# A deformable convolution by shifted products: edge tiles without unasked columns, and a reordered first image

## The chip, the cores and the metric

The kernel runs on one core of one Trainium2 chip, in one launch. The metric is device time in microseconds (us). A profile of one execution stands beside the run times; its engines are PE (TensorE, matmuls; PEld is its weight load), DVE (VectorE), ACT (ScalarE), POOL (GpSimd) and SP (SyncE, which here only issues DMAs). An engine name with a q, as in SPq, is the engine's queue that issues a DMA.

## The reference

The input x has 8 images of 128 channels and 64 x 64 pixels, all float32. Two layers follow each other.

```python
# layer 0
xn   = group_norm(x)                                  # 32 groups
om   = conv3x3(xn, off_w) + off_b                     # 27 maps: 9 taps x (dy, dx), 9 masks
mask = sigmoid(om[:, 18:])
val  = bilinear sample of xn at (row + ky - 1 + dy, col + kx - 1 + dx), per tap, times mask
y    = einsum('bckhw,ock->bohw', val, w) + b
x    = x + relu(batch_norm(y) * gamma + beta)
# layer 1
xn   = group_norm(x)
out  = sum over the two best of four experts (gated per image) of conv3x3(xn, expert) + shared conv3x3(xn)
x    = x + out
```

The change lies in layer 0 alone.

## The kernel before

**Sampling by matmul.** Offsets are assumed to be under 2 pixels (`REACH = 2`; a general path, guarded by a count at the end, is not taken with these inputs). The bilinear weight of a neighbour at distance d is then max(0, 1 - |dy - d|) times the same in x, a "tent", with 5 tents (`NR`) in each direction. The padded image of 66 x 66 sample positions is cut into 11 bands of 6 rows (`NT1`, `T`), and a band into 11 tiles of 6 columns. For one tile, the 10 x 10 source pixels that can matter (`QQ = 100`) stand on the partitions, and the 9 taps x 6 rows x 6 columns = 324 sample positions on the free axis.

- `pick` (L508, L516, ACT) copies the 10 x 10 patches of a band; `pixels` (L529, L536) transposes them on PE into `xt`, pixels by channels.
- `weights` (L546, DVE) multiplies `x_wts` and `y_wts`, the tents of the 100 pixels, into `s` (100 x 324).
- `sample` (L557, PE) multiplies `xt` by `s` into `pq` (128 channels x 324), and ACT (L563) copies it into `samples`, of shape (tap, 8 rows, 66 columns). Two rows are carried to the next band by L665.
- `conv` (L572, PE) adds up 9 products of 6 x 64 columns in `py`, one for each tap, with the tap's 128 x 128 weights. The first band of an image has 4 rows, so 256 columns.
- `finish` (L583, L586) adds the bias, takes statistics and stores the rows.

A float32 matmul is recorded as two instructions; "a pair" below is one such matmul.

**Tables.** `tables(b)` makes the tents of one image: it loads x (L245), normalises it (L257 to L286), computes the offset convolution (L312 to L373) with 32-column products, stores the 27 maps to DRAM by rows (`rowwise`, L378) and, for the x offsets, by columns (`colwise`, after the copy `omc` of L375, stored by L382), loads them shifted by tap into `off_y`, `mask` (L397) and `off_x` (L405), takes the Sigmoid (L413), computes five tents for y (L458 to L463, DVE) and x (L453, L460, ACT), and stores them into `y_table` (L433) and `x_table` (L441). `load_y` (L476) and `load_x` (L492) load a band's tents, 6 and 10 DMAs, into one of two y and three x buffers.

**Order.** The order on every engine is written out by hand. `tables` is a generator; image 0's tables run alone at the start, and those of later images are interleaved, a step or two for each tile, with the band loop. In the loop, at each tile: `weights` three tiles ahead, `sample`, a load for the band after next (from POOL's queue), one tap of `conv` of the band before, and a piece of `pixels` of the next band. At the start the queues are: SP loads x, the offset weights (L596), their bias (L598, four copies) and other constants; POOL clears buffers and combines the offset weights (L612 to L616), then computes the power for `scale` (L279); DVE clears buffers (L391) after the offsets are out. After the tables of image 0, `load_y(0)`, `load_x(0)` (spread over SP, ACT and POOL), `load_y(1)` and `load_x(1)` are issued, then `pick` and `pixels`, and the band loop begins.

Layer 1 (L1159 is its matmul) follows the band loop of all images; its lines do not change.

Of the kernel before, what the change touches and what calls it, by code (L numbers as in the profile page):

```python
# [57 lines left out]
def deform_moe_conv(  # L58
# [110 lines left out]
    def dense():  # L169

        with ExitStack() as st:
# [34 lines left out]

            combos = [a1.tile([P, H // 2, W], F32, name=f"combo{i}") for i in range(2)]
# [6 lines left out]
            )  # L214
            off_x = flat[0:WB, 2 * YSTEP : 2 * YSTEP + TAPS * (WP6 - 1) + ROWPAD]


            x_wts = [a1.tile([P, NT1, T, TAPS, T], F32, name=f"xwts{i}") for i in range(3)]
            y_wts = [a1.tile([P, T, TAPS, WB], F32, name=f"ywts{i}") for i in range(2)]
# [3 lines left out]
            samples = [a1.tile([P, TAPS, T + 2, WB], F32, name=f"samples{i}") for i in range(2)]  # L223
            dw_sb = a1.tile([P, TAPS, P], F32, name="dw_sb")
            ystats = a1.tile([P, B, NT1, 6], F32, name="ystats")
            ymvs = a1.tile([P, B, 2], F32, name="ymvs")
            xts, ss = {}, {}
            bands = [(b, j) for b in range(B) for j in range(NT1)]

            def tables(b):  # L230
# [11 lines left out]
                others = (nc.sync, nc.sync) if b else (nc.scalar, nc.gpsimd)  # L242
# [132 lines left out]
                nc.scalar.copy(omc, omr.rearrange("p (h w) -> p w h", w=W))  # L375
                yield from pause(4)
                for j in range(4):
                    nc.sync.dma_start(  # L378
                        out=rowwise[b][:, j * HW // 4 : (j + 1) * HW // 4],
                        in_=omr[32 * j : 32 * j + 27],  # L380
                    )
                    others[j % 2].dma_start(  # L382
                        out=colwise[b][:, :, H // 4 * j : H // 4 * (j + 1)],
                        in_=omc[32 * j + 9 : 32 * j + 18],
                    )
# [3 lines left out]
                if b == 0:  # L389
                    for t in (y_wts[1], x_wts[1], x_wts[2]):  # L390
                        nc.vector.memset(t, 0.0)  # L391
                yield from pause(9)
                for k in range(3):
                    rows = slice(k, k + H)
                    for t, c in ((off_y, 3 * k), (mask, 2 * TAPS + 3 * k)):
                        one = t[rows, 0, k, 0:1]
                        nc.sync.dma_start(  # L397
                            out=bass.AP(
                                tensor=one.tensor, offset=one.offset,
                                ap=[list(one.ap[0]), [3 * WB + 1, 3], [1, W]],  # L400
                            ),
                            in_=rowwise[b][c : c + 3].rearrange("s (h w) -> h s w", w=W),
                        )
                    one = off_x[rows, k * 3 * (WP6 - 1) + ROWPAD :]
                    others[k % 2].dma_start(  # L405
                        out=bass.AP(
                            tensor=one.tensor, offset=one.offset,
                            ap=[list(one.ap[0]), [WP6, 3], [1, H]],
                        ),
                        in_=colwise[b][k::3].rearrange("s w h -> w s h"),  # L410
                    )
# [3 lines left out]
                if b:  # L415
                    work = a1.tile([WB, 2, 2, YSTEP], F32, name="work", tag="om")
                    tents = [[work[:, a, i % 2] for i in range(NR)] for a in range(2)]
                else:
                    tents = []
                    for t in samples:  # L420
                        flat = t.rearrange("p k r w -> p (k r w)")
                        tents.append(
                            [flat[0:WB, i * YSTEP : (i + 1) * YSTEP] for i in range(NR)]
                        )
# [3 lines left out]
                    ap=[list(one.ap[0]), [T, NT1], [WP6 - 1, TAPS], [1, T]],  # L428
                )

                def store(i):
# [8 lines left out]
                    )  # L440
                    nc.sync.dma_start(  # L441
# [8 lines left out]
                for i in range(NR):  # L450
                    ty, tx = tents[0][i], tents[1][i]
                    step = steps[0:WB, i : i + 1]
                    nc.scalar.activation(  # L453
                        tx.rearrange("p (n k j) -> p n k j", n=NT1, j=T), by_bands, AF.Abs, bias=step
                    )

                    dy, at = off_y.rearrange("p u v j -> p (u v j)"), REACH - i
                    nc.vector.tensor_scalar(ty, dy, -1.0, float(1 - at), ALU.mult, ALU.add)  # L458
                    yield
                    nc.scalar.activation(tx, tx, AF.Relu, bias=1.0, scale=-1.0)  # L460
                    nc.vector.scalar_tensor_tensor(ty, dy, float(1 + at), ty, ALU.add, ALU.min)
                    yield
                    nc.vector.scalar_tensor_tensor(  # L463
                        ty, ty, 0.0, mask.rearrange("p u v j -> p (u v j)"), ALU.max, ALU.mult
                    )
                    if i:
                        store(i - 1)
                    yield from pause(2)
                store(NR - 1)

            def load_y(g, r, engine):

                if g >= len(bands):
# [3 lines left out]
                    out=y_wts[g % 2][r * Q : (r + NR) * Q, r].rearrange("p b c -> p (b c)"),  # L477
# [62 lines left out]
            def weights(n):  # L540

                if n >= len(bands) * NT1:
                    return
                g, c = divmod(n, NT1)
                s = a6.tile([P, TAPS, T, T], F32, name="s")
                nc.vector.tensor_tensor(  # L546
                    s[0:QQ],
                    x_wts[g % 3][0:QQ, c].rearrange("p a k r -> p k r a"),
                    y_wts[g % 2][0:QQ, :, :, T * c : T * c + T].rearrange("p r k a -> p k r a"),
# [4 lines left out]
            def sample(n):  # L554
                g, c = divmod(n, NT1)
                pq = ps_q.tile([P, TAPS, T, T], F32, name="pq")
                nc.tensor.matmul(  # L557
                    pq.rearrange("p k r a -> p (k r a)"),
                    lhsT=xts[g][0:QQ, c],
                    rhs=ss.pop(n)[0:QQ].rearrange("p k r a -> p (k r a)"),  # L560
                    start=True, stop=True,
                )
                nc.scalar.copy(samples[g % 2][:, :, 2 : T + 2, T * c : T * c + T], pq)  # L563

            def conv(g, i, py):
# [4 lines left out]
                n = 3 * kx + ky  # L570
# [4 lines left out]
                    rhs=samples[g % 2][:, n, first + ky : T + ky, kx : kx + W],  # L575
# [20 lines left out]
            nc.sync.dma_start(out=offw_sb[:, :, 0:27], in_=off_w)  # L596
            for j in range(4):
                nc.sync.dma_start(  # L598
                    out=offb_sb[32 * j : 32 * j + 27], in_=off_b.rearrange("a s -> s a")
                )  # L600
            def reach():
# [5 lines left out]
                count = a1.tile([1, 1], F32, name="count")  # L607
                nc.vector.tensor_reduce(count, pn[0:1], AX.X, ALU.add)
                nc.vector.tensor_copy(count_i, count)
# [12 lines left out]
            for _ in made:  # L622
                pass
            for r in range(T):
                load_y(0, r, nc.gpsimd)
            for q in range(Q):
                load_x(0, q, (nc.sync, nc.scalar, nc.gpsimd)[q % 3])
# [4 lines left out]
            for g in range(2):  # L632
                pick(g)
            for _ in pixels(0):
                pass
# [4 lines left out]
            for g in range(len(bands) + 1):  # L640
# [8 lines left out]
                for c in range(NT1):  # L649
# [14 lines left out]
                    if c == 1 and j:  # L664
                        nc.scalar.copy(  # L665
                            samples[g % 2][:, :, 0:2], samples[(g - 1) % 2][:, :, T : T + 2]
# [578 lines left out]
```

## Time and profile before

| what | value |
|---|---|
| median of 3 runs | 1708.23 us (1705.34 to 1708.29) |
| the profiled execution's own time | 1705.5 us |
| its span | 1703.8 us |
| mean granted clock of TensorE | 0.973 |
| first product of `weights` | 75.49 us after the span's start |
| band loop, to the last `conv` | to about 1317 us |

The page's busy shares are over the whole span; its slices are 1/40 of it, 42.6 us each. In a group's line the time after the bar is the busy sum and the mean of one instruction in ns, then the engine's idle time just before these instructions and what ended it. In a timeline the columns are start, duration (both us), engine, line, operation, tiles, and how many were merged.

### The profile page before, as it was taken

What the parts mean: (1) busy time and instruction counts of PE and PEld (TensorE: products, weight loads), DVE (VectorE), ACT (ScalarE), POOL (GpSimd) and SP (SyncE); (2) the same over time, 40 slices, a digit from 0 to 9 for tenths busy, and PEclk for the clock granted to TensorE, in tenths of its full rate; (3) what the DMA queues carried; (4) which work ended last, traced back from release to release, by engine and by line L of the source; (5) the groups of instructions that cost most, each with busy time, mean ns of one, the idle gap of its engine ahead of it and who ended that gap; (6) DMA issues with size and microseconds to landing.
All of it is one profiled execution on the core that took longest, in us unless ns stands there. A gap on an engine that the chain in (4) does not pass through costs nothing. (4 is left out here: it accounts for less than half of the span.)

```text
span 1703.8 us, 20572 instructions
## 1 busy us (share of the span) xinstructions
PE 1591.8 (93%) x6106; PEld 918.3 (54%) x6106; DVE 1280.1 (75%) x1990; ACT 954.9 (56%) x1970; POOL 938.3 (55%) x1518
## 2 busy tenths in 40 slices
PE   3299999999999999999999999999999479999998
PEld 1155565666566556656665665566665234444443
DVE  6586777678687868776786878686664888888882
ACT  1465765776576667657765766676664423333320
POOL 3375576658667757766686676667771412222210
PEclk9599999999999999999999999999999689999999
DMA  4644864685477457647854775675762624444111
GB/s 133 128 119 113 166 169 114 143 183 132 112 159 183 115 120 184 154 114 141 192 125 110 161 183 126 129 162 133 171 149 53 266 87 155 158 153 149 76 63 52
DMA packets 197598, 235.82 MB, mean 138 GB/s; under 512 B 133964, under 2 KB 148048, under 8 KB 197478
## 3 DMA queue, kind: packets, MB, share of 16 engines
q0 software_dynamic: 94976, 124.94, 33.4%
q1 hardware_dynamic: 100556, 109.04, 21.6%
q8 instruction: 54, 0.88, 0.2%
q10 hardware_dynamic: 1946, 0.41, 0.1%
q14 instruction: 66, 0.54, 0.1%
HBM read 183.00 MB, written 50.82 MB: 137 GB/s over the span
## 5 line engine op out<-in xcount | busy, mean ns | idle before, releaser
L546 DVE TENSOR_TENSOR s<-xwts,ywts 100x324 f32<-100x324 f32 x968 | 706.6, 761 | 205.3 <-PE pq L557 172.3
L557 PE MATMUL pq<-s,xt 100*128 100x324 f32 x1936 | 693.5, 440 | 6.0 <-DVE s L546 6.0
L563 ACT COPY samples<-pq 128x324 f32<-128x324 f32 x968 | 425.1, 443 | 410.1 <-PE pq L557 403.5
L572 PE MATMUL py<-samples,dw_sb 128*128 128x384 f32 (+1 forms) x1584 | 624.4, 476 | 0.7 <-ACT y L583 0.7
L492 POOL DMA_DIRECT2D xwts<-tabx x863 | 524.7, 618 | 74.0 <-DMA ywts<-taby 35.9
L476 POOL DMA_DIRECT2D ywts<-taby x528 | 302.9, 588 | 337.2 <-DVE s L546 259.6
L557 PEld LDWEIGHTS pq<-s,xt 100*128 100x128 f32 x1936 | 324.5, 190 | 163.5 <-issue 28.7
L572 PEld LDWEIGHTS py<-samples,dw_sb 128*128 128x128 f32 x1584 | 299.9, 189 | 135.1 <-ACT y L583 2.7
L529 PE MATMUL pt<-ident,picked 128*100 128x128 f32 x968 | 194.6, 276 | 44.2 <-ACT picked L516 34.6
L529 PEld LDWEIGHTS pt<-ident,picked 128*100 128x100 f32 x968 | 121.0, 128 | 186.9 <-issue 44.8
L1159 PE MATMUL pc<-v,u 128*128 128x512 f32 x384 | 172.5, 598 | 9.3 <-DVE u L1108 9.3
L1159 PE MATMUL pc<-v,wmix 128*128 128x512 f32 x384 | 176.0, 604 | 0.0
L536 ACT COPY xt<-pt 100x512 f32<-100x512 f32 (+1 forms) x264 | 147.7, 559 | 2.2 <-PE pt L529 2.2
L1159 PEld LDWEIGHTS pc<-v,u 128*128 128x128 f32 x384 | 72.4, 190 | 98.3 <-issue 85.1
L1137 ACT ACTIVATE t<-pc,bmix 128x512 f32<-128x512 f32 x32 | 22.0, 687 | 182.3 <-PE pc L1159 100.3
L586 DVE BATCH_NORM_STATS2 ystats<-y 128x6 f32<-128x384 f32 (+1 forms) x88 | 48.3, 549 | 100.4 <-ACT y L583 100.4
L1159 PEld LDWEIGHTS pc<-v,wmix 128*128 128x128 f32 x384 | 72.3, 191 | 88.4 <-issue 84.7
L508 ACT COPY picked<-pad 128x900 f32<-128x900 f32 x88 | 91.6, 1041 | 9.6 <-DMA xwts<-tabx 9.6
L665 ACT COPY samples<-samples 128x1188 f32<-128x1188 f32 x80 | 95.9, 1199 | 0.0
L987 POOL TENSOR_TENSOR x<-x,xt 128x512 f32<-128x512 f32 x32 | 47.3, 1514 | 85.0 <-ACT x L985 85.0
L312 DVE TENSOR_TENSOR combo<-pad 128x1024 f32<-128x1024 f32 x64 | 77.4, 1227 | 8.5 <-PE pc L329 8.5
L987 POOL TENSOR_TENSOR pad<-pad,pad 128x512 f32<-128x512 f32 x28 | 39.6, 1445 | 71.7 <-ACT pad L985 71.5
(145 smaller groups left out, 998.3 us busy)
## 6 DMA issues: line engine op xcount, KB each, us to landing
ywts<-taby POOLq DMA_DIRECT2D x528, 116.0 KB, 4.2
pad<-in_x_dram SPq DMA_DIRECT2D x48, 512.0 KB
xwts<-tabx POOLq DMA_DIRECT2D x173, 116.0 KB, 4.1
out_dram<-yo SPq DMA_DIRECT2D x32, 512.0 KB
xwts<-tabx POOLq DMA_DIRECT2D x172, 92.8 KB, 4.0
yd<-y SPq DMA_DIRECT2D x80, 192.0 KB
xwts<-tabx POOLq DMA_DIRECT2D x173, 69.6 KB, 3.7
pad<-yd SPq DMA_DIRECT2D x16, 512.0 KB
```

Source lines behind the costliest of these rows:

```text
L476: engine.dma_start(out=y_wts[g % 2][r * Q : (r + NR) * Q, r].rearrange("p b c -> p (b c)"), in_=bass.AP(tensor=y_table[b].tensor, offset=y ...
L492: engine.dma_start(out=x_wts[g % 3][q:QQ:Q, :, lo:hi].rearrange("p t a b c -> p t (a b c)"), in_=bass.AP(tensor=x_table[b].tensor, offset= ...
L508: nc.scalar.copy(picked[g % 2][:, 1 : NT1 - 1], bass.AP(tensor=one.tensor, offset=one.offset, ap=[list(one.ap[0]), [T, NT1 - 2], [W, Q], [ ...
L529: nc.tensor.transpose(pt[0:QQ, c], picked[g % 2][:, c0 + c].rearrange("p y x -> p (y x)"), ident,)
L536: nc.scalar.copy(xts[g][0:QQ, c0 : c0 + n], pt[0:QQ, 0:n])
L546: nc.vector.tensor_tensor(s[0:QQ], x_wts[g % 3][0:QQ, c].rearrange("p a k r -> p k r a"), y_wts[g % 2][0:QQ, :, :, T * c : T * c + T].rear ...
L557: nc.tensor.matmul(pq.rearrange("p k r a -> p (k r a)"), lhsT=xts[g][0:QQ, c], rhs=ss.pop(n)[0:QQ].rearrange("p k r a -> p (k r a)"), star ...
L563: nc.scalar.copy(samples[g % 2][:, :, 2 : T + 2, T * c : T * c + T], pq)
L572: nc.tensor.matmul(py[:, first:], lhsT=dw_sb[:, 3 * ky + kx], rhs=samples[g % 2][:, n, first + ky : T + ky, kx : kx + W], start=(i == 0), ...
L665: nc.scalar.copy(samples[g % 2][:, :, 0:2], samples[(g - 1) % 2][:, :, T : T + 2])
L987: adder.tensor_tensor(y, y, xt[:, c * CH : (c + 1) * CH], ALU.add)
L1159: nc.tensor.matmul(pc, lhsT=us[j][:, kx], rhs=vs[g][:, rows, kx : kx + W], start=(kx == 0), stop=(kx == 2),)
```

## The change

1. **Edge tiles.** In `samples`, `s` and `pq` the order becomes (row, ky, column, kx), with the taps in reversed order, so that a tile is 18 x 18. `asked` cuts off the two outer rows and columns of this square that no output pixel asks for, in the first and last band and in the first and last tile of a band; the matmul and the copy out take only the rest. `conv` reads its tap from the new layout: the moving operand's column step is 3 elements.
2. The tents and their loads follow the new order (`x_wts` as (column, row, tap), `y_wts` as (row, ky, column, kx)). The y tents are computed in a spare part of `combos[0]`, and the third DVE step writes them in the new order. The offset weights and bias come in reversed tap order: loaded raw into `combos[0]`, reversed by 9 + 9 ACT copies, and the bias sent on by four DMAs.
3. **First image.** The `omc` copy is split between ACT and DVE; the `colwise` stores are all issued by POOL, the `off_x` loads all by ACT; a one-element Sigmoid stands first on ACT; each tent is stored as soon as it is made, x ahead of y; the third x buffer is cleared after the tents; `pick(0)` and `pixels(0)` come ahead of the loads; of `load_x(0)` SP issues six, ACT three, POOL one.

```diff
-            x_wts = [a1.tile([P, NT1, T, TAPS, T], F32, name=f"xwts{i}") for i in range(3)]
-            y_wts = [a1.tile([P, T, TAPS, WB], F32, name=f"ywts{i}") for i in range(2)]
+            x_wts = [a1.tile([P, NT1, T, T, TAPS], F32, name=f"xwts{i}") for i in range(3)]
+            y_wts = [a1.tile([P, T, 3, WB, 3], F32, name=f"ywts{i}") for i in range(2)]
...
-            samples = [a1.tile([P, TAPS, T + 2, WB], F32, name=f"samples{i}") for i in range(2)]
+            samples = [a1.tile([P, T + 2, 3, WB, 3], F32, name=f"samples{i}") for i in range(2)]
+            for t in samples:
+                ends = t.rearrange("p r y w x -> p (r y) (w x)")
+                nc.gpsimd.memset(ends[:, 3 * T :, 0:2], 0.0)
+                nc.gpsimd.memset(ends[:, 3 * T :, 3 * WB - 2 :], 0.0)
...
+            nc.scalar.activation(count_f, nhalf[0:1], AF.Sigmoid)
...
-                nc.scalar.copy(omc, omr.rearrange("p (h w) -> p w h", w=W))
+                turned = omr.rearrange("p (h w) -> p w h", w=W)
+                if b:
+                    nc.scalar.copy(omc, turned)
+                else:
+                    nc.scalar.copy(omc[:, 0 : W // 2], turned[:, 0 : W // 2])
+                    nc.vector.tensor_copy(omc[:, W // 2 :], turned[:, W // 2 :])
...
-                others = (nc.sync, nc.sync) if b else (nc.scalar, nc.gpsimd)
+                beside = nc.sync if b else nc.gpsimd
...
-                    others[j % 2].dma_start(
+                    beside.dma_start(
                         out=colwise[b][:, :, H // 4 * j : H // 4 * (j + 1)],
...
-                    others[k % 2].dma_start(
+                    (nc.sync if b else nc.scalar).dma_start(
...
-                        tx.rearrange("p (n k j) -> p n k j", n=NT1, j=T), by_bands, AF.Abs, bias=step
+                        tx.rearrange("p (n j k) -> p n j k", n=NT1, j=T), by_bands, AF.Abs, bias=step
...
                     nc.vector.scalar_tensor_tensor(
-                        ty, ty, 0.0, mask.rearrange("p u v j -> p (u v j)"), ALU.max, ALU.mult
+                        ty.rearrange("p (v j u) -> p v j u", v=3, u=3),
+                        tent_y.rearrange("p (u v j) -> p v j u", u=3, v=3), 0.0,
+                        mask.rearrange("p u v j -> p v j u"), ALU.max, ALU.mult,
                     )
-                    if i:
-                        store(i - 1)
+                    if b == 0:
+                        store_x(i)
+                        store_y(i)
+                    elif i:
+                        store_y(i - 1)
+                        store_x(i - 1)
...
-                    x_wts[g % 3][0:QQ, c].rearrange("p a k r -> p k r a"),
-                    y_wts[g % 2][0:QQ, :, :, T * c : T * c + T].rearrange("p r k a -> p k r a"),
+                    x_wts[g % 3][0:QQ, c].rearrange("p a r (y x) -> p (r y) a x", x=3),
+                    y_wts[g % 2].rearrange("p r y a x -> p (r y) a x")[
+                        0:QQ, :, T * c : T * c + T
+                    ],
...
+                def asked(t, m0):
+                    m1, k0, k1 = m0 + 3 * T, 0, 3 * T
+                    if j == 0:
+                        m0 += 2
+                    if j == NT1 - 1:
+                        m1 -= 2
+                    if c == 0:
+                        k0 += 2
+                    if c == NT1 - 1:
+                        k1 -= 2
+                    return t[:, m0:m1, k0:k1]
+
+                pq = ps_q.tile([P, 3 * T, 3 * T], F32, name="pq")
                 nc.tensor.matmul(
-                    pq.rearrange("p k r a -> p (k r a)"),
+                    asked(pq, 0),
                     lhsT=xts[g][0:QQ, c],
-                    rhs=ss.pop(n)[0:QQ].rearrange("p k r a -> p (k r a)"),
+                    rhs=asked(ss.pop(n)[0:QQ].rearrange("p m a x -> p m (a x)"), 0),
                     start=True, stop=True,
                 )
-                nc.scalar.copy(samples[g % 2][:, :, 2 : T + 2, T * c : T * c + T], pq)
+                rows = samples[g % 2].rearrange("p r y w x -> p (r y) (w x)")
+                nc.scalar.copy(
+                    asked(rows[:, :, 3 * T * c : 3 * T * (c + 1)], 6), asked(pq, 0)
+                )
...
-                    rhs=samples[g % 2][:, n, first + ky : T + ky, kx : kx + W],
+                    rhs=samples[g % 2][:, first + ky : T + ky, 2 - ky, kx : kx + W, 2 - kx],
...
-            nc.sync.dma_start(out=offw_sb[:, :, 0:27], in_=off_w)
+            nc.sync.dma_start(out=raw_w.rearrange("p k s t -> p k (s t)"), in_=off_w)
+            nc.sync.dma_start(out=raw_b.rearrange("p s t -> p (s t)"), in_=off_b)
...
+            for k in range(TAPS):
+                nc.scalar.copy(reversed_w[:, :, :, k], raw_w[:, :, :, TAPS - 1 - k])
+            for k in range(TAPS):
+                nc.scalar.copy(reversed_b[:, :, k], raw_b[:, :, TAPS - 1 - k])
             for j in range(4):
-                nc.sync.dma_start(
-                    out=offb_sb[32 * j : 32 * j + 27], in_=off_b.rearrange("a s -> s a")
-                )
+                nc.sync.dma_start(out=offb_sb[32 * j : 32 * j + 27], in_=offb_row)
...
+            pick(0)
+            for _ in pixels(0):
+                pass
             for r in range(T):
                 load_y(0, r, nc.gpsimd)
             for q in range(Q):
-                load_x(0, q, (nc.sync, nc.scalar, nc.gpsimd)[q % 3])
+                load_x(0, q, (nc.sync, nc.sync, nc.scalar)[q % 3] if q < 9 else nc.gpsimd)
+            pick(1)
             for r in range(T):
                 load_y(1, r, nc.gpsimd)
             for q in range(Q):
                 load_x(1, q, nc.sync)
-            for g in range(2):
-                pick(g)
-            for _ in pixels(0):
-                pass
```

## The prediction

> **What bounds the kernel now.** I read the page's busy table and slices first, then TensorE's timeline inside one band, then the groups of the deform stage by shape, then the timeline of the first 80 us.
>
> ```profile
> PE 1591.8 (93%) x6106; PEld 918.3 (54%) x6106; DVE 1280.1 (75%) x1990; ACT 954.9 (56%) x1970; POOL 938.3 (55%) x1518
> PE   3299999999999999999999999999999479999998
> PEclk9599999999999999999999999999999689999999
> ```
>
> The digits show two places where PE is not full: the first two slices (the first image's tables, up to about 80 us) and the seam near 1320 us before layer 1. A busy digit 9 doesn't prove a full PE, so I look at the order of its starts:
>
> ```profile
> 627.61 0.71 PE L557 MATMUL pq<-s,xt 100*128 100x324 f32 x2
> 628.16 0.81 PE L572 MATMUL py<-samples,dw_sb 128*128 128x384 f32 x2
> 628.81 0.38 PE L529 MATMUL pt<-ident,picked 128*100 128x128 f32 x2
> 629.02 0.71 PE L557 MATMUL pq<-s,xt 100*128 100x324 f32 x2
> 629.57 0.81 PE L572 MATMUL py<-samples,dw_sb 128*128 128x384 f32 x2
> 630.22 0.71 PE L557 MATMUL pq<-s,xt 100*128 100x324 f32 x2
> 630.77 0.81 PE L572 MATMUL py<-samples,dw_sb 128*128 128x384 f32 x2
> ```
>
> Start to start, a pair of pq (324 columns) takes 0.55 us, a pair of py (384 columns) 0.65 us, one transpose 0.11 us. So 60 columns cost 0.10 us: **1.67 ns a column of a pair**, and nothing is left between them. A band has 11 pq, 9 py and 11 pt: 6.05 + 5.85 + 1.2 = 13.1 us, and the same place in the next band is 13.05 us later. In this stage every column removed from PE is time removed from the run, and every nanosecond added per column is added.
>
> ```profile
> L546 DVE TENSOR_TENSOR s<-xwts,ywts 100x324 f32<-100x324 f32 x943 | 689.0, 762 | 186.3 <-PE pq L557 171.5 <-DMA xwts<-tabx 9.5 <-DMA ywts<-taby 2.2
> L563 ACT COPY samples<-pq 128x324 f32<-128x324 f32 x947 | 416.1, 443 | 396.1 <-PE pq L557 389.6
> L665 ACT COPY samples<-samples 128x1188 f32<-128x1188 f32 x79 | 94.7, 1199 | 0.0
> L312 DVE TENSOR_TENSOR combo<-pad 128x1024 f32<-128x1024 f32 x56 | 68.1, 1227 | 6.5 <-PE pc L329 6.5
> L375 ACT COPY om<-om 128x1024 f32<-128x1024 f32 x7 | 14.1, 2011 | 0.0
> ```
>
> DVE and ACT wait for pq, not the other way round. The group also prices strides. L375 reads with a step of 256 bytes: 2011 ns for 1024 elements, 1.96 ns each; L665 reads rows: 1.01 ns each. L546 reads xwts with a step of 216 bytes: 2.35 ns an element; L312 reads rows: 1.20 ns. One element in each distant place costs about double.
>
> ```profile
> 46.54 1.28 ACT L413 ACT_TABLE_LOAD   x1 [11.79 <-DMA combo<-rowwise]
> 57.35 0.29 SPq L433 DMA_DIRECT2D taby<-samples  x1
> 57.74 0.84 SPq L441 DMA_DIRECT2D tabx<-samples  x1
> 61.73 15.48 SPq L492 DMA_DIRECT2D xwts<-tabx  x13
> 62.56 3.43 POOL L476 DMA_DIRECT2D ywts<-taby  x6 [19.70 <-DMA tabx<-samples]
> 75.49 4.73 DVE L546 TENSOR_TENSOR s<-xwts,ywts 100x324 f32<-100x324 f32 x7 [18.16 <-DMA ywts<-taby]
> ```
>
> Before 75.49 us the run is one serial chain: offsets, mask, tents, stores, loads, first product. Each step shortened there counts in full too.
>
> **What the Trainium skill says.** *SBUF — State Buffer*, Door 1, says that SBUF has 16-byte lines, that an engine needs at least two hits per line for full rate, and sums it up as "how far you can stride for free depends on dtype: 4 fp32". The trace agrees far beyond a line (216 and 256 bytes: double). For a step of 12 bytes the two sentences part: it is under 4 fp32, but gives 4 elements in 3 lines, fewer than two hits. No row of before has such a step. *ScalarE: Activation LUTs*, What ACT_TABLE_LOAD costs, gives about 1283 ns; the trace has 1.28 us.
>
> **The change, part by part.**
>
> *Edge products.* A tile's product has 18 rows by 18 columns; edge tiles lose 2 on each outer side. An image's 11 x 11 tiles go from 121 x 324 = 39,204 columns to (198 - 4) squared = 37,636: 1,568 fewer, 12,544 over 8 images, x 1.67 ns = **-20.9 us**, all on the path. The smallest edge product has 256 columns, and py with 256 columns runs in L572 too, so weight loads (190 ns) stay covered. L563 copies 16 x 16 to 18 x 18 elements, never more than before. Rows of 16 out of 18 in PSUM are not contiguous; L329 already writes rows of 63 out of 64 there. Bound: 0 to -21.
>
> *Taps innermost.* To make that rectangle, samples becomes (row, ky, column, kx), so the convolution's moving operand steps 3 floats, **12 bytes**, instead of 1. It streams 36,864 columns an image (10 bands of 9 x 384, one of 9 x 256), 294,912 in all, 492 us. Bounds: 0 if a step under a line is free; if a line takes two element times, 3 lines per 4 elements is 6 times instead of 4: +246 us; doubled as at 216 bytes: +492. Below nothing is excluded: the rows read now are contiguous. I take 0, because the page's summary puts the limit at 4 fp32 and because the doubling is shown only where each element has its own line.
>
> *L546* now reads runs of 3 and 18 instead of a 216-byte step: between 0.43 (324 x 1.2 ns plus its overhead) and 0.76 us. DVE waits for PE there, so it is worth nothing in the steady stage; its cover is PE.
>
> *Tents.* For every image the third DVE tent step reads both inputs with a large step (0.77 up to 1.4 us by the doubling), ACT's Abs as well (0.80 up to 1.3). For images 1 to 7 that is 7 x 5 x 1.1 us beside a full PE, with DVE idle some 20% of the stage: nothing; were DVE full, 39 us.
>
> *First image, early.* Weights come raw and ACT reverses them: 9 copies, then 9 of the bias, at 0.2 us each (two L516 copies take 0.40). The weights land near 9.5 us (SP's beta load at 9.52 had waited for them), so they are ready near 11.3 instead of POOL's start of L612 at 10.46; the pow of `scale` is queued behind on POOL and slips 0.8 us. Four small memsets on POOL lie inside that. The bias is ready near 13.1; SP issues four more DMAs (2.46 us for such four) and they land near 17, while the first combo, due at 16.2, overwrites the raw buffer: 0.8 more. SP's later loads for image 1 slip about 5 us; image 1 is first needed at 82. Together **+1.6** (0 to +3).
>
> *First image, middle.* The Sigmoid table at the start takes 1.28 off 46.54. The omc copy split over ACT and DVE gives colwise 0.9 us, and four colwise stores on POOL instead of two return it (0.94 each); both lie beside SP's six off_y/mask loads, which end last. ACT issues three off_x loads instead of two, 0.7 us, before the Sigmoid it has to wait for anyway. The memset of x_wts[2] moves behind the tents, where DVE waits for loads. Against it five slower third steps, +3.1, move the last y store from 57.35 to 59.2; but now y goes last and x, whose 726 small rows land slowest (57.74 to 61.7), goes earlier. I take **-0.3** (-3 to +2).
>
> *First image, loads.* Before, POOL issues six y loads, then three of the first band's x loads from 65.95 to 68.6, which need about 7 us to land: 75.5. After, POOL has one of these, SP six ahead of the next band's, ACT three behind pick and pixels. The last is issued near 66: first product near 73, **-2.5** (-5 to +1).
>
> Sum: -20.9 + 1.6 - 0.3 - 2.5 = -22.1. The profiled execution took 1705.5 us (span 1703.8), giving 1683.4; the median shown is 2.7 above it, giving 1686. I say 1685.
>
> **Rivals.**
>
> *The 12-byte step is charged.* L572 alone gets slower: at 1.5 times 1705.5 - 22 + 246 = **1930 us**, at double 2175. It decides from 22/492 = 4.5%: a py pair of 0.68 instead of 0.65 us. For it speaks the two-hits sentence; against it that only steps far above a line are seen to cost. 0.18.
>
> *Another engine sets the edge bands.* A top or bottom band shrinks by 0.5 us to about 12.5, POOL issues 16 loads of 0.6 us in it, 9.7, and waits for DVE in between (L476). If half the gain is lost there: **1695 us**. Against: loads are issued two bands ahead. 0.10.
>
> *The first image gets later instead of earlier,* 5 us, by the small copies and slower tents: **1690 us**; speaks for it that they are serial. 0.12. Eaten up altogether, about 1706: 0.03.
>
> **How the numbers follow.** Forecast 0.57, and the two milder rivals 0.10 and 0.12, are all faster by over 0.2% (3.4 us, about what a measurement of this kernel tells from no change): 0.79. No difference 0.03. Slower 0.18. The range 1674 to 1699 takes in the ends of the first image's terms and the half-lost edge gain; the charged step lies outside it.
>
> **What would show it.** Right: pq pairs of 0.48 us at edges (288 columns) and 0.43 at corners, py pairs still 0.65, no table load before the Sigmoid, first L546 product near 73, layer 1 unchanged. Wrong: py pairs over 0.68 us, or PE waiting for POOL's loads in top and bottom bands, or the first combo later than 17 us.

## The result: 1957 us, the opposite of the forecast, and the profile after

| what | before | after |
|---|---|---|
| median of 4 runs | 1707.89 us (1705.34 to 1708.29) | 1957.37 us (1956.06 to 1958.25) |
| ratio after / before | | 1.1464, interval 1.1444 to 1.1484 |
| span of the profiled execution | 1703.8 us | 1956.2 us |
| mean granted clock of TensorE | 0.973 | 0.976 |
| first product of `weights` | 75.49 us | 76.53 us |
| last `conv` of the band loop done | about 1317 us | about 1571 us |

The change costs 249.5 us. The clock is the same, and of the span's 252 us the band loop has all (its end moves by 254). The page of after, the lines that answer to those shown of before:

```profile
PE 1851.2 (95%) x6106; PEld 934.3 (48%) x6106; DVE 1049.1 (54%) x1991; ACT 977.1 (50%) x1988; POOL 935.4 (48%) x1521
...
PE   3499999999999999999999999999999947999998
...
PEclk8699999999999999999999999999999978999999
```

PE is busy 1851 us instead of 1592, with the same 6106 matmul instructions; DVE and POOL have not become busier, and ACT only by 22 us (977 instead of 955). So the time is inside PE's own instructions. PE's timeline inside one band of after shows which:

```profile
700.82 0.72 PE L606 MATMUL pq<-s,xt 100*128 100x324 f32 x2
701.37 1.19 PE L623 MATMUL py<-samples,dw_sb 128*128 128x384 f32 x2
702.39 0.39 PE L561 MATMUL pt<-ident,picked 128*100 128x128 f32 x2
...
703.17 1.18 PE L623 MATMUL py<-samples,dw_sb 128*128 128x384 f32 x2
...
704.29 0.65 PE L606 MATMUL pq<-s,xt 100*128 100x288 f32 x2
704.78 1.18 PE L623 MATMUL py<-samples,dw_sb 128*128 128x384 f32 x2
```

Start to start, a pair of pq is what it was (0.55 us for 324 columns, 0.49 for an edge tile's 288), but a pair of py takes 701.37 to 702.39 = **1.02 us instead of 0.65**. The groups of after (columns: count, then busy us and mean ns of one, then idle time before and its releaser) say the same over the whole run:

```profile
L623 PE MATMUL py<-samples,dw_sb 128*128 128x384 f32 (+1 forms) x1584 | 911.1, 660 | 0.7 <-ACT y L634 0.7
L606 PE MATMUL pq<-s,xt 100*128 100x324 f32 (+2 forms) x1936 | 675.7, 430 | 14.9 <-DVE s L578 14.9
...
L578 DVE TENSOR_TENSOR s<-xwts,ywts 100x324 f32<-100x324 f32 x968 | 461.1, 492 | 587.0 <-PE pq L606 557.6
```

The convolution waits for almost nothing (0.7 us), and DVE, whose product became quicker (762 to 492 ns), waits for PE 558 us where it waited 172. A faster helper has only gained idle time.

### The profile page after: what moved, and what is told of

Same layout as the page of the kernel before. It is cut to its first block, busy times and chain, and to the rows that moved or that the text cites. A ratio compares the mean times of both kernels' runs of the same rounds, so it can differ in the third digit from the quotient of the medians.

```text
span 1956.2 us, 20279 instructions
## 1 busy us (share of the span) xinstructions
PE 1851.2 (95%) x6106; PEld 934.3 (48%) x6106; DVE 1049.1 (54%) x1991; ACT 977.1 (50%) x1988; POOL 935.4 (48%) x1521
## 5 line engine op out<-in xcount | busy, mean ns | idle before, releaser
L623 PE MATMUL py<-samples,dw_sb 128*128 128x384 f32 (+1 forms) x1584 | 911.1, 660 | 0.7 <-ACT y L634 0.7
L578 DVE TENSOR_TENSOR s<-xwts,ywts 100x324 f32<-100x324 f32 x968 | 461.1, 492 | 587.0 <-PE pq L606 557.6
L613 ACT COPY samples<-pq 128x324 f32<-128x324 f32 (+2 forms) x968 | 408.4, 423 | 654.4 <-PE pq L606 645.6
L606 PE MATMUL pq<-s,xt 100*128 100x324 f32 (+2 forms) x1936 | 675.7, 430 | 14.9 <-DVE s L578 14.9
L606 PEld LDWEIGHTS pq<-s,xt 100*128 100x128 f32 x1936 | 332.3, 194 | 329.7 <-issue 226.9
L561 PEld LDWEIGHTS pt<-ident,picked 128*100 128x100 f32 x968 | 128.9, 134 | 260.4 <-issue 185.5
L324 DVE TENSOR_TENSOR combo<-pad 128x1024 f32<-128x1024 f32 x64 | 76.9, 1218 | 17.3 <-PE pc L341 11.2
```

Source lines behind the costliest of these rows:

```text
L561: nc.tensor.transpose(pt[0:QQ, c], picked[g % 2][:, c0 + c].rearrange("p y x -> p (y x)"), ident,)
L578: nc.vector.tensor_tensor(s[0:QQ], x_wts[g % 3][0:QQ, c].rearrange("p a r (y x) -> p (r y) a x", x=3), y_wts[g % 2].rearrange("p r y a x - ...
L606: nc.tensor.matmul(asked(pq, 0), lhsT=xts[g][0:QQ, c], rhs=asked(ss.pop(n)[0:QQ].rearrange("p m a x -> p m (a x)"), 0), start=True, stop=True,
L613: nc.scalar.copy(asked(rows[:, :, 3 * T * c : 3 * T * (c + 1)], 6), asked(pq, 0))
L623: nc.tensor.matmul(py[:, first:], lhsT=dw_sb[:, 3 * ky + kx], rhs=samples[g % 2][:, first + ky : T + ky, 2 - ky, kx : kx + W, 2 - kx], sta ...
```

## The experiments

Each ratio is against runs of before on the same chip. There were three chips for the experiments (e1 to e4 on one, e5 to e8 on another, e9 and e10 on the third), and the median of before is 1704.2, 1700.6 and 1703.8 us on them. So where two experiments from different chips are compared, the distance of each from its own before is given too.

### 1. Is it the 12-byte step, and the step alone?

*e1_unit_step*: after, and the convolution reads neighbouring floats.

```diff
-                    rhs=samples[g % 2][:, first + ky : T + ky, 2 - ky, kx : kx + W, 2 - kx],
+                    rhs=samples[g % 2].rearrange("p r y w x -> p r y (w x)")[
+                        :, first + ky : T + ky, 2 - ky, 6 + kx : 6 + kx + W
+                    ],
```

> The changed kernel, but conv reads 64 neighbouring floats of the same rows (step 1) instead of every third: other sample values, so not the reference's result, with the same number of columns. Theory 1, the 12-byte step of the moving operand is the whole loss: a py pair returns from 1.02 to 0.65 us and the run to about 1957 - 768 x 0.365 x 384-column pairs (about 275 us) = 1684 us (1678 to 1692). Theory 2, something else in the new layout or the edge rectangles slows PE (rows of 16 out of 18 in PSUM, ACT writing samples where PE reads them): py stays above 0.8 us and the run above 1850.

*e3_before_step3*: before, and only the step of the convolution's read becomes 3 floats.

```diff
+                one = samples[g % 2][:, n, first : first + 1, 0:1]
...
-                    rhs=samples[g % 2][:, n, first + ky : T + ky, kx : kx + W],
+                    rhs=bass.AP(
+                        tensor=one.tensor, offset=one.offset,
+                        ap=[list(one.ap[0]), [WB, T - first], [3, W]],
+                    ),
```

> The kernel before with one edit: conv's moving operand takes every third float of its tap's rows (other values, so not the reference's result; same columns). Theory 1 (the step alone): py pairs of 1.02 us as in the changed kernel, 295,000 columns x (1.02 - 0.65)/384 = 281 us, so about 1985 us. Theory 2 (the step is harmless and the layout is to blame): 1708 us.

*e6_full_tiles*: after, with the four `if`s of `asked` taken out, so that every tile is 18 x 18.

> The changed kernel with full 18 x 18 products and copies for every tile. Here conv's slow step keeps PE full, so that nothing else can bind at the edges: if a column of pq costs 1.67 ns wherever PE binds, this is 20.9 us slower than the changed kernel, 1978 us. If rows of 16 out of 18 cost more in PSUM than whole rows, it is less than 15 us slower.

Measured: e1 **1709.68 us**, ratio 1.0028 (1.0010 to 1.0046); e3 **1970.27**, 1.1565 (1.1545 to 1.1584); e6 **1979.92**, 1.1627 (1.1589 to 1.1666). One line of PE's timeline and the start of the next give the pair, first in e1, then in e3:

```profile
701.94 0.81 PE L623 MATMUL py<-samples,dw_sb 128*128 128x384 f32 x2
702.59 0.65 PE L606 MATMUL pq<-s,xt 100*128 100x288 f32 x2
```

```profile
699.79 1.18 PE L573 MATMUL py<-samples,dw_sb 128*128 128x384 f32 x2
700.80 0.39 PE L529 MATMUL pt<-ident,picked 128*100 128x128 f32 x2
```

The pair is back at 0.65 us without the step, and takes 1.01 us with it. One address step put into before costs 266 us; the same step taken out of after gives back 248 (244, if each is taken from its own before). e3 stays 15 us under the 1985 that were expected. e1 is not at the 1678 to 1692 us of its first theory: the pair is right, but some 25 us are lost elsewhere, and part 3 looks for them.

The edge crop, which is what the edge tiles leave out, is worth 1979.92 - 1957.37 = 22.6 us by the medians, where PE is the bound (29.8 from each one's own before). The traces narrow it down: from the last bias addition of image 0 to that of image 7, after takes 1293.0 us and e6 1310.4, so 17.3 us for seven images or **about 20 for eight** (20.9 was forecast). So 266 - 20 = 246 of the 249.5 us are named. The few that are left are of the size by which chips and single executions differ.

### 2. What does a step cost? The law in one table

*e4_steps*: before, with a tail of matmuls, copies and products put between layer 1 and the end, each on 384 elements whose places step by 1, 2, 3, 4, 5, 8 or 16 floats.

```diff
+            for k in (1, 1, 1, 1, 2, 3, 4, 5, 8, 16, 1):
+                p = qp.tile([P, N], F32, name="mm" + names[k], tag="mm")
+                for _ in range(8):
+                    nc.tensor.matmul(p, lhsT=lhs, rhs=stepped(src, k), start=True, stop=True)
```

> The kernel before, with a tail after layer 1 that does nothing but read one buffer of ones at steps 1, 2, 3, 4, 5, 8 and 16 floats: 8 matmuls of 384 columns each, an ACT copy and a DVE product of 384 elements each, then the same two with 2 to 8 distant rows read in turn, and ACT copies that turn a PSUM tile of 18 x 18. No other engine uses SBUF beside it for long. Theory 1a (a 16-byte line costs about 1.76 ns, elements of one line are free up to the port's rate): matmul pairs of 0.65 us at step 1, 0.67 at step 2 (half a line an element, 0.88 ns), 1.02 at step 3, 1.35 from step 4 on. Theory 1b (a cliff: any step above 8 bytes costs the same): 0.65 at 1 and 2, 1.02 at 3, 4, 5, 8. Theory 1c (any step but 1 is charged): 1.02 from step 2 on. ACT should follow the same law[...]; DVE too if the law is the memory's and not the engine's.

The groups of the probe in e4 (16 instructions are 8 pairs; the mean of one includes overlap with its neighbour):

```profile
L1220 PE MATMUL mmeight<-src,lhs 128*128 128x384 f32 x16 | 11.2, 868 | 0.0
...
L1220 PE MATMUL mmfour<-src,lhs 128*128 128x384 f32 x16 | 11.0, 853 | 0.0
L1220 PE MATMUL mmthree<-src,lhs 128*128 128x384 f32 x16 | 8.3, 674 | 0.0
L1220 PE MATMUL mmtwo<-src,lhs 128*128 128x384 f32 x16 | 5.6, 499 | 0.0
```

From the starts in the timeline (8 pairs of step 3 from 1728.0 to 1736.1 us, of step 4 to 1746.9, of step 5 to 1757.9, of step 8 to 1768.9, of step 16 to 1779.2), and the copies and products, one instruction for each step:

| step, floats | 1 | 2 | 3 | 4 | 5 | 8 | 16 |
|---|---|---|---|---|---|---|---|
| PE, us a pair of 384 columns | 0.65 | 0.675 | 1.01 | 1.35 | 1.37 | 1.38 | 1.29 |
| ACT copy, ns | 511 | 540 | 715 | 878 | 903 | 917 | 888 |
| DVE product, ns | 536 | 553 | 674 | 850 | 866 | 882 | 856 |

A pair is two passes of 384. At a step of 4 floats each element has its own 16 bytes: 1.35 us / 768 = 1.76 ns. At 3 floats there are 3 such lines for 4 elements: 0.75 x 1.76 = 1.32 ns, and 1.01 us / 768 is 1.32. At 2 floats half a line: 0.88 ns, and 0.675 / 768 is 0.88. At 1 float it is 0.85 instead of a quarter line's 0.44, so there the element is the limit. **A new 16-byte line costs about two elements' time; beyond 16 bytes nothing more is charged.** So theory 1a is what came; the cliff of 1b and the charge on every step of 1c are out. ACT and DVE have the same shape: little from step 1 to 2, a steady rise to 4, nothing more after it. Of the two sentences in *SBUF — State Buffer*, Door 1, in the Trainium skill, the one that asks for at least two hits on a line fits these numbers, and the summary of "4 fp32" does not: of steps under four floats, two is nearly free and three is not. The probe has no other engine writing what PE reads and still shows 1.01 us at step 3, so a clash of PE's reads with ACT's writes isn't needed to explain after.

*e10_before_step2*: e3 with a step of 2 floats, to see whether the law holds in the kernel.

```diff
-                        ap=[list(one.ap[0]), [WB, T - first], [3, W]],
+                        ap=[list(one.ap[0]), [WB, T - first], [2, W]],
```

> Kernel before, the convolution's read of samples with a step of two floats (8 bytes) in place of one, nothing else (so the values it convolves are others). Theory (16-byte lines, the law that the probe showed: 0.65, 0.675, 1.01, 1.35 us a pair for steps of 1, 2, 3, 4 floats): a pair in the convolution 0.025 us longer, 792 pairs: +19.8 us where TensorE is what ends the work: 1.009 to 1.014. Rival (any step other than one is charged in the kernel, since samples are being written meanwhile, so that the probe is too kind): a pair of 0.75 or more, over 1.04.

Measured 1727.54 us, 1.0136 (1.0110 to 1.0163), so +23.7 for 792 pairs, 0.030 us each against the probe's 0.025; the interval takes in the 19.8 us that were expected. The law holds in the kernel (pairs take 0.68 to 0.69 us there).

### 3. Why is the kernel not faster once the step is gone?

e1 has the edge crop and a unit step, and is still not faster than before. *e2_unit_step_full_tiles* is e1 with full tiles; it asks how much of the crop e1 keeps.

> As the unit-step kernel (conv reads neighbouring floats, so not the reference's result), but every product and copy takes all 18 x 18 of a tile. If the edge columns were wholly on the path at 1.67 ns each, this is 20.9 us slower than the unit-step kernel with edge rectangles, about 1705 us, and all of the gain over before is the edge. If another engine took over at the edges, the difference is about half, 10 us. What is left between this one and before is the first image: 0 to +2 us slower, since its first product came at 76.5 instead of 75.5 us.

Measured 1723.21 us, 1.0110 (1.0093 to 1.0127). About 1705 was expected, so this missed as well. The crop brings only 1723.21 - 1709.68 = 13.5 us there, between the 20.9 and the 10 of the two cases, and what remains of the change costs 19 us over before (1704.2 in these runs). So the loss is not at the edges. The waits of e1 between 100 and 1310 us (engine, line, what it waited for: us, times, longest) point at the tents:

```profile
PE pt L561 <- ACT xt L568: 24.7, 15, 5.1
...
ACT combo L430 <- DMA combo<-rowwise: 12.0, 5, 4.4
```

PE, which in after waits for ACT nowhere in this stretch, waits up to 5.1 us at a time for ACT's `xt` copies. Before has 6.7 us of this in all:

```profile
PE pt L529 <- ACT xt L536: 6.7, 14, 1.2
```

ACT makes an x tent in two steps, Abs and Relu, and DVE a y tent in three. The groups by shape show what became of Abs and of DVE's third step, first in before, then in after:

```profile
L453 ACT ACTIVATE work<-combo,steps 66x594 f32<-66x594 f32 x35 | 28.5, 816 | 7.5 <-DMA tabx<-work 7.4
L463 DVE SCALAR_TENSOR_TENSOR work<-work,combo 66x594 f32<-66x594 f32 x35 | 27.0, 771 | 3.9 <-ACT combo L413 3.8
```

```profile
L473 ACT ACTIVATE work<-combo,steps 66x594 f32<-66x594 f32 x35 | 49.0, 1400 | 0.0
L485 DVE SCALAR_TENSOR_TENSOR work<-combo,combo 66x594 f32<-66x594 f32 x35 | 29.1, 832 | 13.3 <-ACT combo L430 13.2
```

Abs, which now goes round nine rows (one for each tap), went from 816 to 1400 ns; DVE's third step, which goes round three, only from 771 to 832.

*e5_unit_step_abs_rows*: e1, and Abs reads rows again (the x tents then stand in the order of before).

```diff
-                    ap=[list(one.ap[0]), [T, NT1], [1, T], [WP6 - 1, TAPS]],
+                    ap=[list(one.ap[0]), [T, NT1], [WP6 - 1, TAPS], [1, T]],
...
-                        tx.rearrange("p (n j k) -> p n j k", n=NT1, j=T), by_bands, AF.Abs, bias=step
+                        tx.rearrange("p (n k j) -> p n k j", n=NT1, j=T), by_bands, AF.Abs, bias=step
```

> The unit-step kernel with one more edit: ACT's Abs of the x tents runs in the old order (tap, row) and reads off_x in rows again, so the x tents stand in another order (other values, not the reference's result; same counts). The unit-step kernel is 5 us over before instead of 21 under it; its PE is idle 24.7 us behind L568 on ACT in the tents of images 1 to 7. Theory 3: the strided Abs (1.40 instead of 0.80 us, 5 for each image) fills ACT there and delays L568: then this kernel is 12 to 20 us faster than the unit-step kernel (1685 to 1697). Rival: ACT is held by the Sigmoid's wait for its DMAs, which the shorter edge bands reach sooner: then it gains less than 6 us (1703 or more) and the waits before L430 stay near 15 us.

Measured **1688.62 us**, 0.9931 (0.9909 to 0.9953). That is 12.0 us under its before, where e1 was 5.5 over its own: 17.5 us (21 by the medians) for 40 instructions that together got 23 us shorter. Where it comes from is seen by taking the start of each band's bias addition (`y<-py`) from the timelines, 88 in a run. The table has the mean time in us from the band before to the one named, over images 1 to 6. The next image's tents fall into bands 5 to 7 (counted from 0).

| kernel | band 4 | bands 5 to 7 together | band 9 |
|---|---|---|---|
| before | 13.03 | 39.99 | 13.02 |
| after | 16.30 | 48.90 | 15.63 |
| e2, full tiles | 13.10 | 42.73 | 13.07 |
| e1 | 12.97 | 43.94 | 12.30 |
| e5, Abs in rows | 12.98 | 41.14 | 12.33 |

In after three bands take exactly 3 x 16.3: the slow convolution hides the tents. In e2 they take 2.74 us more than in before, 7 x 2.74 = 19 us, as much as all of e2's loss. From e1 to e5 it is 2.80, or 19.6 us for seven images. The first image adds to it (its first product comes at 77.67 us in e1 and at 73.20 in e5), since Abs holds up its stores too. The two together are more than the 17.5 to 21 us of the runs; the traced execution of e1 was the slowest of its nine (1717.77 us).

So Abs is most of the loss, but not all of it. In e5 bands 5 to 7 are still 1.15 us above before, and PE still waits 12.2 us for `xt`. The rival, the Sigmoid's wait for its loads (the second line of e1 above), holds ACT as well: it went from 12.0 to 5.5 us together with Abs, and no run takes it away alone. In e9 below neither of the two is left.

### 4. A version that keeps the gain

*e7_turned_copy*: what after computes, with a unit step: `samples` becomes (row, ky, kx, column), and ACT's copy out of PSUM turns (column, kx) into (kx, column); the edge tiles need a second, small copy.

```diff
-            samples = [a1.tile([P, T + 2, 3, WB, 3], F32, name=f"samples{i}") for i in range(2)]
+            samples = [a1.tile([P, T + 2, 3, 3, WB], F32, name=f"samples{i}") for i in range(2)]
...
+                    nc.scalar.copy(
+                        rows[:, 6 + m0 : 6 + m1, xs, T * c + a_lo : T * c + a_hi],
+                        pq.rearrange("p m (a x) -> p m a x", x=3)[:, m0:m1, a_lo:a_hi, xs].rearrange("p m a x -> p m x a"),
+                    )
```

> The changed kernel, computing the same: samples is laid out (row, ky, kx, column), so that conv reads in steps of 1, and the copy out of PSUM turns (column, kx) into (kx, column), reading PSUM in steps of 3 floats and writing runs of 6; edge tiles of a band take a second small copy. From the probe the copy costs 0.44 us either way (0.71 if it wrote scattered instead). Expected like the unit-step kernel, 1705 to 1712 us; above 1725 if PSUM reads at a step of 12 bytes cost ACT more in company of PE's writes.

Measured 1714.67 us, 1.0072 (1.0045 to 1.0098), with bands 5 to 7 at 43.25: the step is gone, the tents remain. It is 9 us further above its before than e1, and above the 1705 to 1712 expected; the second copies keep ACT busy for 35 us, and whether they are the cause was not tested. In the probe of e4 ACT's turning copy of 324 elements took 440 ns when it read PSUM at a step of 12 bytes and wrote runs of six, as long as a plain one, and 712 when it wrote the scattered side.

*e8_turned_copy_dve_tents*: e7, and for images 1 to 7 Abs reads rows, while a DVE step takes the place of ACT's Relu and turns the order there (one more small DVE step turns the mask's sign); the loads of x and the Sigmoid stand at other places in the order.

```diff
-                    nc.scalar.activation(tx, tx, AF.Relu, bias=1.0, scale=-1.0)
+                    if b:
+                        nc.vector.tensor_scalar(
+                            tx.rearrange("p (n j k) -> p n j k", n=NT1, j=T),
+                            tent_x.rearrange("p (n k j) -> p n k j", n=NT1, j=T),
+                            1.0, 1.0, ALU.min, ALU.subtract,
+                        )
+                    else:
+                        nc.scalar.activation(tx, tx, AF.Relu, bias=1.0, scale=-1.0)
```

> The turned-copy kernel with the two other losses taken away, computing the same: for images 1 to 7 ACT's Abs reads in rows and DVE, which idles 35% there, takes the place of ACT's Relu and turns the order (min(t,1) - 1, with the mask's sign turned too), which frees 1.3 us of ACT a tent; and the four x loads of an image stand one step closer, the Sigmoid four steps later after its loads. If theory 3 and its rival together are what is lost: 1684 us (1680 to 1692), 1.2% under before. If PE still waits: about 1700.

Measured 1707.65 us, 1.0038 (1.0022 to 1.0054), where 1680 to 1692 was expected. PE's waits between 100 and 1310 us say where the turning went:

```profile
PE pq L627 <- DVE s L599: 9.2, 22, 0.8
PE pt L582 <- ACT xt L589: 5.1, 7, 0.8
```

In e7 PE waited 23.0 us for ACT's `xt` and never for DVE's `s`. Now it waits for DVE, whose new step takes 1222 ns; bands 5 to 7 stand at 42.10. Image 0, whose Abs still goes round nine rows, has its first pq at 77.63 us. Which of e8's edits cost most was not taken apart.

*e9_rows_only*: gives up the column crop to have no turning anywhere. `s` and `pq` become (row, ky, kx, column) with a plain copy into the layout of e7, only the first and last band leave out two rows, Abs reads rows, the y offsets are loaded in their final order.

```diff
-                    if c == 0:
-                        k0 += 2
-                    if c == NT1 - 1:
-                        k1 -= 2
...
-                    rhs=samples[g % 2][:, first + ky : T + ky, 2 - ky, kx : kx + W, 2 - kx],
+                    rhs=samples[g % 2][:, first + ky : T + ky, 2 - ky, 2 - kx, kx : kx + W],
```

> The computation of after, full result, put together from what the runs before have shown to be free: samples laid out (row, ky, kx, column), so that the convolution reads a unit step; s and pq in the order (row, ky, kx, column), so that the first and last band leave out two of their 18 rows and no tile leaves out columns; both tents in the order of before (Abs over rows of off_x, vertical distances loaded in their final order, so no reordering on VectorE); the first image's changes as in after. Theory: the two causes found (the 12-byte step, and ACT's longer Abs in images 1 to 7 once TensorE is fast) are all that was lost, so the saving that is left shows: 22 tiles of an image x 36 columns x 8 images x 1.67 ns = 10.6 us on TensorE, and the first product some 2.5 us earlier (73.75 us in the kernel with unit step and Abs in rows): 1690 to 1697 us, ratio 0.992 to 0.996, py pair 0.65, ACT's wait at the tents (PE pt from ACT xt) 7 us or less. Rival: what kept the version with turned copies at 1707 lies in the layout of samples itself (a row of 66 floats beside eight others), which this kernel shares: 1702 to 1708, ratio 1.000 to 1.003.

Measured **1690.11 us** (1684.82 to 1693.75), 0.9916 (0.9892 to 0.9939): 0.8% faster than before, as the theory said (1690 to 1697). Its page, its waits and its first image's timeline:

```profile
PE 1584.6 (94%) x6106; PEld 919.8 (54%) x6106; DVE 1254.5 (74%) x1991; ACT 951.6 (56%) x1988; POOL 935.0 (55%) x1517
```

```profile
PE pt L555 <- ACT xt L562: 3.5, 9, 0.6
```

```profile
56.10 0.77 SPq L446 DMA_DIRECT2D taby<-samples  x1
...
62.38 3.39 POOL L502 DMA_DIRECT2D ywts<-taby  x6 [24.19 <-DMA xwts<-tabx]
...
72.97 6.01 DVE L572 TENSOR_TENSOR s<-xwts,ywts 100x324 f32<-100x324 f32 x9 [14.29 <-DMA ywts<-taby]
```

PE is busy 1584.6 us, the wait at the tents is half of before's, ACT's Sigmoid waits nowhere in this stretch, and bands 5 to 7 take 39.75. The gain is 13.7 us (10 to 18 by the interval). The rows left out, two in each of 22 tiles of an image, are worth 10.6 us by the price of 1.67 ns a column; in the traces images 1 to 7 take 1061.2 us instead of 1069.3, so 8.1 where 9.3 are priced. The rest was not taken apart. The first product, at 72.97, is earlier than in any trace with before's start, but by 0.6 to 2.5 us only, and the part behind the band loop (the span less the start of the last bias addition), which nothing here changes, takes between 382.6 and 386.8 us from run to run. DVE's product is back at 736 ns, and PE doesn't wait for it.

## Why the prediction was wrong, point by point

**The step that failed is "Taps innermost": "I take 0".** It should have been the bound that stands beside it, +246: the step costs 266 us in e3, and taking it out of after gives back 244 to 248. The prediction had the arithmetic, 3 lines for 4 elements and 1.5 times the time, and the point of decision, a py pair of 0.68; the pair is 1.02. Its rival "The 12-byte step is charged" gave 1930 us at a chance of 0.18, and 1957 came. Two sentences of one page disagreed; I chose the summary over the mechanism, although this term's bound was ten times any other term and the strided rows that the trace had (L375, L546) were charged. The reason given, that these are far above a line, was no evidence for a step below it. The small misfit, 1.56 times instead of 1.5, is that a line's price is 1.76 ns, a little more than two elements' of 0.85.

**Edge products: right.** About 20 us by the traces (22.6 by the medians) where PE is the bound, against 20.9; pq pairs of 0.49 us for 288 columns. But "all on the path" holds only while PE never waits: with the unit step the crop brought 13.5 (e1, e2).

**Tents, images 1 to 7: "nothing" was right in after, but by luck.** After hides them, since its PE is a quarter slower per band, for a reason that the forecast had put at nothing. With PE at the speed that the prediction assumed they cost 19 us (e2, bands 5 to 7). The prediction's escape, "were DVE full, 39 us", named the wrong engine: DVE's step had been priced up to 1.4 us and took 0.83, while Abs, priced up to 1.3, took 1.40, and ACT is the engine whose `xt` copies PE then waits for. ACT is busy 56% of before's span, and still has a few microseconds in which it has nothing to spare.

**L546 (now L578):** 492 ns, inside 0.43 to 0.76 us, and worth nothing, as said.

**First image.** The timeline of after:

```profile
0.79 1.28 ACT L238 ACT_TABLE_LOAD   x1 [0.79 <-PEq L1285]
...
9.57 1.36 ACT L656 COPY offw_sb<-combo 128x27 f32<-128x27 f32 x9 [7.29 <-DMA combo<-in_off_w_dram]
...
16.36 4.63 DVE L324 TENSOR_TENSOR combo<-pad 128x1024 f32<-128x1024 f32 x4 [0.46 <-ACT pad L297]
...
58.23 0.59 SPq L450 DMA_DIRECT2D taby<-samples  x1
...
64.47 3.39 POOL L508 DMA_DIRECT2D ywts<-taby  x6 [27.38 <-DMA xwts<-tabx]
...
76.53 2.53 DVE L578 TENSOR_TENSOR s<-xwts,ywts 100x324 f32<-100x324 f32 x6 [15.94 <-DMA ywts<-taby]
```

- *Early, +1.6:* the nine copies end at 10.93 (11.3 forecast), POOL starts at 11.01 instead of 10.46, and the first combo at 16.36 instead of 15.39: **+1.0** in these two traces. It waits for `pad`, not for the bias DMAs out of the raw buffer; that 0.8 did not arise. And it did not last: the offset convolution is done at 32.25 us, against 32.78 before.
- *Middle, -0.3:* Sigmoid's table is loaded at 0.79, and the Sigmoid itself starts at 46.58, where the table load of before stood (46.54): the 1.28 us are gained. They are lost again in the tents, which take ACT 2.0 us each instead of 1.43. DVE has its last y tent ready at 56.87, but the store of it stands in SP's queue behind the last x store, which waits for ACT, so that it is issued at 58.23 instead of 57.35 (59.2 forecast, from DVE steps that took 0.83 us and not 1.4).
- *Loads, -2.5:* the assumption that x's stores hold up the loads, so that y can go last, was wrong. POOL's first y loads begin at 62.56 in before. The profile's line names an x store (tabx) as what they waited for, but the loads of x that wait for the last x store go out only at 63.7, so it was the last y store, issued at 57.35. In after y is last in the queue: its store goes out at 58.23, the y loads begin at 64.47, and the first product stands at 76.53, not at 73.

Two traces are thin ground here, and the other runs widen it. With before's start the first product stands at 73.53 to 75.49 us (before, e3, e4, e10), with the new start and the nine-row Abs at 76.12 to 78.67 (after, e1, e2, e6, e7, e8), with the new start and Abs in rows at 73.20 and 72.97 (e5, e9). In the mean the new start is 2.8 us late, where the three terms together promised 1.2 early. In e1 and e5, which differ by Abs alone, the slower Abs is what costs it; without it the gain is about 1 us.

**What would show it:** pq pairs as said (0.49), no table load before the Sigmoid, layer 1 unchanged (its two groups of matmuls keep 173 and 176 us), and py pairs over 0.68, the sign named as the one that proves it wrong.

## What to carry to other kernels

Before a layout is turned to save columns, count the 16-byte lines that every reader of it touches, TensorE's moving operand first: here 4% fewer columns in one matmul cost 56% more time in another. Where two bounds of a term differ by ten times the expected gain, the term is the forecast, and it is worth a probe of a few matmuls. Put a turn, if one is needed, where an engine reads PSUM and writes runs (440 ns in the probe, against 712 for scattered writes), and then look again at the waits, because an engine that had been hidden behind the slow one may set the pace.

## What was not expected of the hardware

- Going round two or three distant rows costs much less than going round four or more. With 384 elements that cycle over 2, 3, 4, 6 and 8 rows 1024 bytes apart, ACT took 645, 671, 899, 893 and 896 ns, against 511 for neighbouring elements; DVE took 612, 641, 881, 877 and 878, against 536 (e4, one instruction each). So it matters how many lines are in turn, and not only how far they lie apart; it fits Abs (nine rows, 1.7 times) and DVE's third step (three rows, 1.08 times).
- Reading PSUM at a step of 12 bytes cost ACT nothing in the probe (440 ns for 324 elements, as for a plain copy) and little in the kernel (455 ns in e7, 438 in e1). PE's writing of 16 of 18 rows or columns there cost nothing either (1.70 ns a column at 288 and at 324 columns).
- A step of 16 bytes costs as much as one of 32 or 64 (1.35, 1.38 and 1.29 us a pair): the step's price does not grow any further once each element has its own line.
